# Four small edits in a four-layer image kernel: mask building, first row norm, scaling, and joint-stage statistics

## The chip, the cores and the metric

The kernel runs on one core of a Trainium2 chip, as one program. The metric is device time in microseconds (us) of that core. Engines are named as in the profile: PE (TensorE matmul), PEld (weight loads), DVE (VectorE), ACT (ScalarE), POOL (GpSimd), SP (SyncE, which here only issues DMAs).

## What is computed

Eight images of 56×56 pixels and 192 channels, f32, go through four residual layers, x = x + layer(gn(x)), where gn is a group norm over 32 groups of 6 channels of a whole image:

```python
x = x + L0(gn(x))   # silu(q)*silu(v), Toeplitz mix along rows and columns, gate, output projection
x = x + L1(gn(x))   # LN; shifted-window attention, 7x7 windows, 6 heads, bias + mask; projection
x = x + L2(gn(x))   # W_in (192->384); 3x3 depthwise conv; four EMA scans; LN over 384; W_out
x = x + L3(gn(x))   # 7x7 depthwise conv; LN; 192->768, gelu, 768->192; scaled

# L1, the mask: 64 windows, 49x49 each
attn = einsum(q * scale, k) + bias[None] + mask[None, :, None];  softmax
# L2
proj = x @ W_in + b_in;   local = conv3x3(proj)
mixed = 0.25 * (lr + rl + tb + bt) + local          # scans of local, decay 0.6
out = layernorm_over_channels(mixed) @ W_out + b_out
```

The group norm of a layer needs statistics of the whole image, so every layer's statistics are gathered while the residual of the layer before is added.

## The kernel before

A framework allocates tiles from pools with a number of buffers each, sets the waits from tile to tile, and orders the instructions of each engine, except where the kernel fixes an order itself. Each engine runs its own queue strictly in order. A tile with `bufs=1` can be rewritten only when everything that reads it is done, a DMA out of it included; pools with `bufs=2` and no own number in the call give two buffers. In the profile the stages lie one after another: 0 to 870 q/v projection, 876 to about 2097 the Toeplitz mix, to 3441 attention, 3470 to 3757 layer 2's input projection, to 4385 the depthwise mix, to 4905 the joint stage (layer 2's end with layer 3's beginning), to 5228 the 7×7 convolution, and to 6118 the MLP. The change touches four of them.

**Masks (`build_bias_mask`, L301 to L336).** During the q/v projection (`layer0_qv`: matmuls L371, evacuation with the bias L377 on DVE, silu L378 on ACT, product L379 on DVE), the sums of bias and mask that the attention will add are built in eight chunks and kept in DRAM (`bmask`). Chunk g: POOL clears a tile `mk` (L326) and issues two loads of the mask into it (L328); DVE adds the bias of each of six heads, six instructions (L331), into `bmt`; POOL issues the store to `bmask` (L334). Both `mk` and `bmt` have one buffer. The driver takes chunks from a list (`masks`) between row steps of the projection; in the order that the framework makes of it, all eight stand close together, from 234 to 302 us.

**First norm of the attention (`layer1_norm`, L622 to L662).** A generator for one image, in four row groups g of 392 columns: it scales x (ACT L636), subtracts a mean found by matmul (L644, DVE L646), squares it (ACT L648), sums the squares by matmul (L652) and copies 32 partitions of sums into `rs` (L653). After all four rows comes one square root (ACT L654, with a table load), one reciprocal (DVE L655), then per row a matmul that spreads the factors (`rstd`, L660) and the multiplication (DVE L662). For image 0 the whole generator runs ahead of the first attention block (L1266 to L1269). For the others it is advanced by the letter N of a hand-written plan (L1278), a list of parts whose order PE follows: Q projects queries and keys (L679), V values (L698), E makes weights (scores, max, exp, sum, normalise; L719 to L734; the POOL multiplications L729 and L734 are in it), T transposes them (L754), P multiplies with v, R projects. The parts of image 0's first block run ahead of the plan (L1272 to L1274).

**Input projection (`layer2_in`, L811 to L843; called at L1323 to L1328).** For image b: POOL clears the padding of `xn` (L815), DVE scales the image in three instructions (L818), POOL clears two edge rows (L821, L822), then 15 groups of matmuls (L830) write PSUM tiles `pin` (four buffers), each evacuated with the bias by DVE (L838) into `pt`; at the end SP stores `pt` to `pd` (L843). The next image's load (`layer2_image`, SP, L807 and L808) is issued ahead of it. `x`, `xn` and `pt` have two buffers. After image 5 the last image's group norm is finished (`gn_finish`, L168 to L182), as its sums come last from the attention.

**Joint stage (`layer2_out`, `layer3_in`, loop in the driver).** DVE's order is written out by hand there: the order of the code. An image has 12 places i = 3k + j (four column groups k, three channel groups j). At each: normalised rows `yt` for the next group (DVE L951, ACT L953), the output projection (PE L975), the residual on DVE (L980, into x2o), and pieces of two other chains. One is the layer norm statistics of the next image (`ln_pieces`, DVE L190 on `ml`, 28 pieces of 0.87 us), at i = 3 to 8, and its variance at i = 8. The other is the generator `layer3_in` of the image before: group norm statistics (L144, 12 instructions of 0.55 us), group norm finish (L168 and after), scaling (POOL L1000), transposes (PE L1015) and copies (ACT L1023 to L1027), and the store `zd` (L1028). It is advanced by one step at places i < 5, two from i = 5 on. The transposed normalised rows are copied by ACT into `y` (L963). The load of `ml` for image b+2 is issued on SP at k = 3.

The functions that the diff touches, and what calls them:

Of the kernel before, what the change touches and what calls it, by code (L numbers as in the profile page):

```python
# [10 lines left out]
F32 = mybir.dt.float32  # L11
# [9 lines left out]
TT = 392  # L21
# [56 lines left out]
def kernel(ctx: ExitStack, tc: tile.TileContext, a: dict, out: bass.AP):  # L78
# [222 lines left out]
    def build_bias_mask(psum, pool, masks):  # L301


        rev = pool.tile([WN, WN], F32, name="rev", bufs=1)
        nc.gpsimd.dma_start(rev, a["rev49"])

        raw = pool.tile([WN, HEADS, WN], F32, name="raw", bufs=1)
        tab = a["rel"]
        for i in range(7):
            for h in range(HEADS):  # L310
                nc.gpsimd.dma_start(
                    raw[7 * i:7 * i + 7, h].rearrange("p (i j) -> p i j", i=7),
                    bass.AP(tab.tensor, tab.offset + 13 * i + 169 * h, [[1, 7], [13, 7], [1, 7]]),
                )
        yield
        bt = pool.tile([128, HEADS, WN], F32, name="bt", bufs=1)
        nc.vector.memset(bt, 0.0)
        bp = psum.tile([128, 2, 512], F32, name="bp", tag="qv")[0:WN, 0, 0:HEADS * WN]
        nc.tensor.matmul(bp, rev, raw.rearrange("p h m -> p (h m)"), start=True, stop=True)
        for r in range(2):  # L320
            nc.vector.tensor_copy(bt[64 * r:64 * r + WN].rearrange("p h m -> p (h m)"), bp)
        mask = a["mask"].rearrange("(g q r) n m -> g r n q m", q=4, r=2)

        def eighth(g):
            mk = pool.tile([128, 4, WN], F32, name="mk", bufs=1)
            nc.gpsimd.memset(mk, 0.0)  # L326
            for r in range(2):
                nc.gpsimd.dma_start(mk[64 * r:64 * r + WN], mask[g, r])  # L328
            bm = pool.tile([128, 3, 4, 2, WN], F32, name="bmt", bufs=1)
            for h in range(HEADS):  # L330
                nc.vector.tensor_tensor(  # L331
                    bm[:, h % 3, :, h // 3, :], mk, bt[:, h:h + 1, :].to_broadcast([128, 4, WN]), ALU.add
                )
            nc.gpsimd.dma_start(bmask[g], bm.rearrange("p a b c d -> p (a b c d)"))  # L334

        masks += [lambda g=g: eighth(g) for g in range(8)]  # L336


    def layer0_load(b, pool):
# [279 lines left out]
        rolled(x1[b], x, False, queues)  # L619
        return x  # L620

    def layer1_norm(b, x, pool, psum, consts):  # L622


        ones2, ones32, sel = consts[4:]

        xr = pool.tile([128, 3 * NH + 16], F32, name="xr")
        nc.gpsimd.memset(xr[:, 3 * NH:], 0.0)
        xw = xr[:, 0:3 * NH].rearrange("p (j n) -> p j n", j=3)
        rs = pool.tile([128, TT], F32, name="rs1")  # L630
        yield xr
        sc, sh = scsh1[:, b, 0], scsh1[:, b, 1]
        for g in range(4):
            gs = bass.ts(g, TT)
            for j in range(3):
                nc.scalar.activation(  # L636
                    xw[:, j, gs].rearrange("p (w i j) -> p w i j", i=7, j=7),
                    x[:, j, 7 * g:7 * g + 7].rearrange("p i (w j) -> p w i j", j=7), AF.Identity,
                    bias=sh[:, j:j + 1], scale=sc[:, j:j + 1],
                )  # L640
# [12 lines left out]
            nc.vector.tensor_copy(rs[32 * g:32 * g + 32], vp)  # L653
        nc.scalar.activation(rs, rs, AF.Sqrt, bias=eps5)  # L654
        nc.vector.reciprocal(rs, rs)  # L655
        for g in range(4):
            yield
            gs = bass.ts(g, TT)
            bp = psum.tile([128, 512], F32, name="rstd", tag="mm", bufs=3)[:, 0:TT]
            nc.tensor.matmul(bp, sel[32 * g:32 * g + 32], rs[32 * g:32 * g + 32], start=True, stop=True)  # L660
            xs = xw[:, :, gs]
            nc.vector.tensor_tensor(xs, xs, bp.unsqueeze(1).to_broadcast([128, 3, TT]), ALU.mult)  # L662

    def layer1_scores(g, xr, pool, psum, S, es, consts):

# [142 lines left out]
        queue.dma_start(x[64:128, :, 0:R2 - 3], src[:, :, R2 - 1:H])  # L808
        return x

    def layer2_in(b, x, pool, psum, w_in, b_in):  # L811

        sc, sh = scsh2[:, b, 0], scsh2[:, b, 1]
        xn = pool.tile([128, 3, R2, 64], F32, name="xn2")
# [5 lines left out]
            ))  # L820
        nc.gpsimd.memset(xn[0:64, :, 0, 0:W], 0.0)  # L821
        nc.gpsimd.memset(xn[64:128, :, R2 - 3:R2, 0:W], 0.0)  # L822
        pt = pool.tile([128, C2, P2], F32, name="pt")
        nh = R2 // 2
        for i in range(nh):
            ns = 2 if i + nh < P2 else 1
            ps = psum.tile([128, 2, 512], F32, name="pin")
            for j in range(3):
                for s in range(ns):
                    nc.tensor.matmul(  # L830
                        ps[:, s, 0:C2], xn[64 * s:64 * s + 64, j, 2 * i:2 * i + 2].rearrange("p h w -> p (h w)"),
                        w_in[64 * s:64 * s + 64, j], start=(j == 0), stop=(j == 2),
                    )
# [4 lines left out]
            nc.vector.tensor_tensor(dst, ps[:, 0:ns, 0:C2], b_in[:, v, 0:ns], ALU.add)  # L838

        n = CG2 if b + 1 == nimg else 0  # L840
        if n:
# [123 lines left out]
                bias=vec("be2", m), scale=vec("g2", m),  # L965
            )

    def layer2_out(k, j, y, x, psum, w_out):
# [12 lines left out]


    def layer3_in(b, x, zp, pool, psum):
# [260 lines left out]
    with ExitStack() as st:  # L1244
# [30 lines left out]

# [6 lines left out]
        for b in range(nimg):  # L1282
# [5 lines left out]
            for g in range(4):  # L1288
# [27 lines left out]
    with ExitStack() as st:  # L1316
# [3 lines left out]
        x = [layer2_image(0, xpool, nc.scalar)]  # L1320
        w_in = resident("w_in", nc.scalar, pool)
        b_in = resident("b_in", nc.scalar, pool)
        for b in range(nimg):  # L1323
            if b + 1 < nimg:
                x.append(layer2_image(b + 1, xpool, nc.sync))
            layer2_in(b, x[b], pool, psum, w_in, b_in)
            if b == nimg - 3:
                run(gn_finish(mv2[:, last], scsh2[:, last, 0], scsh2[:, last, 1], pool, psum, "pin"))  # L1328
    with ExitStack() as st:
# [29 lines left out]
        for n in range(-1, len(groups)):  # L1359
# [9 lines left out]
            for j in range(3):  # L1369
# [2 lines left out]
                        rows[0] = ln_rows(*var_next, eps5, pool)  # L1372
                    following = scaled(*after, j)
                if n >= 0:
                    layer2_out(k, j, y, x[b], psum, w_out)
# [10 lines left out]
            if k == 3:  # L1386
                run(steps)
                nc.sync.dma_start(xd[b], x[b])
                steps = layer3_in(b, x[b], zp, pool, psum)
        run(steps)  # L1390


# [133 lines left out]
```

## Time and profile before

| | |
|---|---|
| three runs | 6127.48, 6127.55, 6136.09 us; median 6127.55 |
| the profiled execution | 6119.55 us |
| its span | 6117.8 us, mean granted PE clock 0.943 |
| POOL busy | 1330.2 us (22%) |
| DMA moved | 1013 MB, mean 166 GB/s |
| input projection, 8 blocks | 3469.8 to 3756.7 |
| joint stage, period of an image | 58.4 us (4658.4 to 4716.8 to 4775.2) |

How to read it: the page gives busy times over the whole span; of an edit to one stage they tell little, because the stages have different limits. The groups of instructions ("line engine operation, out<-in, shapes, count | busy, mean ns | idle before <-releaser") tell how long an instruction takes and what it waited for. The windows give the busy times of a stretch with the granted PE clock. The waits give "engine tile line <- releaser: total us, times, longest".

### The profile page before, as it was taken

What the parts mean: (1) busy time and instruction counts of PE and PEld (TensorE: products, weight loads), DVE (VectorE), ACT (ScalarE), POOL (GpSimd) and SP (SyncE); (2) the same over time, 40 slices, a digit from 0 to 9 for tenths busy, and PEclk for the clock granted to TensorE, in tenths of its full rate; (3) what the DMA queues carried; (4) which work ended last, traced back from release to release, by engine and by line L of the source; (5) the groups of instructions that cost most, each with busy time, mean ns of one, the idle gap of its engine ahead of it and who ended that gap; (6) DMA issues with size and microseconds to landing.
All of it is one profiled execution on the core that took longest, in us unless ns stands there. A gap on an engine that the chain in (4) does not pass through costs nothing. (4 is left out here: it accounts for less than half of the span.)

```text
span 6117.8 us, 126576 instructions
## 1 busy us (share of the span) xinstructions
PE 5451.9 (89%) x55636; PEld 3509.4 (57%) x55636; DVE 3401.5 (56%) x4760; ACT 2216.8 (36%) x2938; POOL 1330.2 (22%) x867
## 2 busy tenths in 40 slices
PE   6799989999999888888888687999889889799999
PEld 5576766666666545555555455677544489444444
DVE  5677765565555445455454475888787601433331
ACT  2344444444444333333332101555466610333333
POOL 2100015444445212222222101433201100110100
PEclk8899999999999888999998898999989999899999
DMA  6799986666666614544533475667667588321210
GB/s 163 185 214 215 194 224 260 251 258 257 253 255 259 124 33 65 66 61 65 61 50 53 119 227 192 228 231 236 196 166 223 171 319 326 118 88 58 84 48 24
DMA packets 1034540, 1013.11 MB, mean 166 GB/s; under 512 B 826136, under 2 KB 958196, under 8 KB 1007220
## 3 DMA queue, kind: packets, MB, share of 16 engines
q1 hardware_dynamic: 1019424, 940.93, 54.5%
q0 software_dynamic: 8416, 39.40, 2.0%
q10 hardware_dynamic: 6148, 24.68, 1.3%
q8 instruction: 437, 7.16, 0.5%
q14 instruction: 115, 0.94, 0.0%
HBM read 676.28 MB, written 345.08 MB: 167 GB/s over the span
## 5 line engine op out<-in xcount | busy, mean ns | idle before, releaser
L371 PE MATMUL qv<-w_qv_sb,xn 64*112 64x288 f32 x5376 | 724.6, 426 | 51.1 <-DVE act L377 47.8
L409 POOL COPY lc<-lt 128x896 f32<-128x896 f32 (+1 forms) x320 | 572.7, 1806 | 620.4 <-PE op L417 602.6
L371 PEld LDWEIGHTS qv<-w_qv_sb,xn 64*112 64x112 f32 x5376 | 532.7, 184 | 238.1 <-DVE act L377 64.4
L378 ACT ACTIVATE act<-act 112x576 f32<-112x576 f32 x448 | 300.3, 682 | 462.1 <-DVE act L377 424.4
L1154 PE MATMUL ph<-y,w_sb 64*128 64x392 f32 x2304 | 398.4, 498 | 6.4 <-ACT hid L1158 6.4
L1165 PE MATMUL po<-hid,w_sb 128*64 128x392 f32 x2304 | 386.3, 494 | 0.0
L429 PE MATMUL pj<-xn,w_p_sb 64*128 64x392 f32 (+1 forms) x1920 | 373.4, 515 | 13.8 <-issue 10.5
L417 PEld LDWEIGHTS op<-rc,lc 128*56 128x56 f32 x9216 | 308.1, 136 | 127.1 <-issue 66.1
L417 PE MATMUL op<-rc,lc 128*56 128x56 f32 x9216 | 339.4, 221 | 43.9 <-POOL lc L409 25.7
L450 PE MATMUL y<-pp,w_o_sb 128*64 128x392 f32 (+1 forms) x1920 | 356.2, 504 | 21.9 <-DVE x L458 12.7
L377 DVE TENSOR_TENSOR act<-qv,b_qv 112x576 f32<-112x576 f32 x448 | 320.8, 751 | 90.8 <-PE qv L371 90.4
L1172 DVE TENSOR_TENSOR x<-x,z 128x392 f32<-128x392 f32 x96 | 71.0, 740 | 522.1 <-ACT z L1170 522.1
L409 ACT COPY rc<-rt 128x896 f32<-128x896 f32 (+1 forms) x160 | 256.8, 1605 | 238.7 <-PE op L417 219.8
L881 PE MATMUL cv<-zc,wt 128*128 128x224 f32 x1536 | 312.8, 355 | 24.2 <-DMA zc<-pd 24.2
L881 PEld LDWEIGHTS cv<-zc,wt 128*128 128x128 f32 x1536 | 290.2, 189 | 67.8 <-issue 51.9
L443 DVE TENSOR_TENSOR pp<-pp,ot 128x784 f32<-128x784 f32 (+1 forms) x160 | 154.6, 966 | 313.2 <-ACT pp L434 293.7
L1154 PEld LDWEIGHTS ph<-y,w_sb 64*128 64x128 f32 x2304 | 220.3, 188 | 176.3 <-issue 26.2
L729 POOL TENSOR_TENSOR e<-e,mx 128x1176 f32<-128x1176 f32 x64 | 139.8, 2184 | 812.5 <-DVE mx L728 629.6
L1055 PE MATMUL cps<-zc,wt 128*128 128x224 f32 x1536 | 299.1, 355 | 16.7 <-DMA zc<-zd 15.6
L830 PE MATMUL pin<-w_in_sb,xn 64*128 64x384 f32 x1392 | 251.5, 511 | 60.4 <-POOL xn L821 60.4
L1055 PEld LDWEIGHTS cps<-zc,wt 128*128 128x128 f32 x1536 | 289.0, 189 | 26.9 <-issue 19.4
L679 PE MATMUL qk_ps<-xr,wg 64*96 64x392 f32 x1536 | 299.5, 511 | 0.3 <-ACT oa L780 0.3
(211 smaller groups left out, 9113.6 us busy)
## 6 DMA issues: line engine op xcount, KB each, us to landing
lt<-left SPq DMA_DIRECT2D x72, 1792.0 KB
rt<-right SPq DMA_DIRECT2D x72, 1792.0 KB
left<-qv SPq DMA_DIRECT2D x224, 252.0 KB
right<-qv SPq DMA_DIRECT2D x448, 126.0 KB
wt<-in_band_dram SPq DMA_DIRECT2D x23, 2048.0 KB
wt<-in_band_dram SPq DMA_DIRECT2D x11, 4096.0 KB
zc<-pd SPq DMA_DIRECT2D x187, 232.0 KB
pd<-pt SPq DMA_DIRECT2D x7, 5568.0 KB
```

The lines of the kernel that those rows point to most:

```text
L371: nc.tensor.matmul(ps[s][:, which, 0:D1 // 2], xn[64 * s:64 * s + 64, j, bass.ts(i, 2 * W)], w_qv[64 * s:64 * s + 64, j, which, ns], start ...
L377: nc.vector.tensor_tensor(act, ps[s][:, :, 0:D1 // 2], b_qv[:, :, ns], ALU.add)
L378: nc.scalar.activation(act, act, AF.Silu)
L409: copy(c[:, 0:nu], raw.rearrange("p (w u d) -> p u d w", u=nu, d=64 // nu)[:, :, d0:d0 + 8])
L417: nc.tensor.matmul(op[64 * u:64 * u + W, i, :], lc[:, u, i], rc[:, u, i], start=True, stop=True)
L429: nc.tensor.matmul(ps[0:M, s, 0:TT], w_p[64 * s:64 * s + 64, j, d0:d0 + M], xn[64 * s:64 * s + 64, j, ts], start=(j == 0), stop=(j == 2),)
L450: nc.tensor.matmul(y[64 * s:64 * s + 64], w_o[0:M, c, 64 * j:64 * j + 64], pp[0:M, s], start=(c == gated[0][0]), stop=(c == gated[-1][0]),)
L679: nc.tensor.matmul(ps[s], wg[64 * s:64 * s + 64, j, c0:c0 + HC], xw[64 * s:64 * s + 64, j, gs], start=(j == 0), stop=(j == 2),)
L881: nc.tensor.matmul(dst, wt[:, c4 + i, 128 * q:128 * q + 128], zc[:, :, c4 + i, q:q + NPAIR], start=(q == 0), stop=(q == 1),)
L1055: nc.tensor.matmul(dst.rearrange("p (b n) -> p b n", n=NPAIR), wt[:, c4 + i, q * OP:(q + 1) * OP], zc[:, :, c4 + i, q:q + NPAIR], start=(q ...
L1154: nc.tensor.matmul(ps[:, s, 0:TT], w0[64 * s:64 * s + 64, j, m * 128:(m + 1) * 128], y[64 * s:64 * s + 64, j, ts], start=(j == 0), stop=(j ...
L1165: nc.tensor.matmul(ps[64 * s:64 * s + 64], w1[:, m, 64 * j:64 * j + 64], hid[:, m, s], start=(m == 0), stop=(m == 5),)
```

## The change

It makes four edits.

1. The mask tile gets two buffers; the load of chunk g + 1 is issued ahead of chunk g's additions, and that of chunk 0 when the list is made. `bmt` stays at one buffer.
2. For image 0, each row of `layer1_norm` takes its own square root (straight from PSUM) and reciprocal over 32 partitions, and is scaled at once. The first block's Q parts begin after row 0, and the other rows are advanced between parts and by N.
3. The scaling of layer 2's input (with its three memsets) is a function of its own, run for image b + 1 after the evacuation i = 7 of image b.
4. In the joint stage the group norm's statistics are taken from each residual tile right behind it (nine instructions of 448 columns and three of 224, in place of twelve of 392), so that `layer3_in` loses them and two of its steps. The next image's layer norm pieces lie over places i = 1 to 8, three or four at each; two generator steps are taken from i = 6 on, not 5.

```diff
-        def eighth(g):
-            mk = pool.tile([128, 4, WN], F32, name="mk", bufs=1)
+        def load(g):
+            mk = pool.tile([128, 4, WN], F32, name="mk")
             nc.gpsimd.memset(mk, 0.0)
             for r in range(2):
                 nc.gpsimd.dma_start(mk[64 * r:64 * r + WN], mask[g, r])
+            mks.append(mk)
+
+        def add(g):
             bm = pool.tile([128, 3, 4, 2, WN], F32, name="bmt", bufs=1)
...
-        masks += [lambda g=g: eighth(g) for g in range(8)]
+        load(0)
+        masks += [lambda g=g: (load(g + 1) if g < 7 else None, add(g)) for g in range(8)]
```

```diff
@@ layer1_norm(b, x, pool, psum, consts, first=False)
+        def scaled(g):
+            gs = bass.ts(g, TT)
+            bp = psum.tile([128, 512], F32, name="rstd", tag="mm", bufs=3)[:, 0:TT]
+            nc.tensor.matmul(bp, sel[32 * g:32 * g + 32], rs[32 * g:32 * g + 32], start=True, stop=True)
+            xs = xw[:, :, gs]
+            nc.vector.tensor_tensor(xs, xs, bp.unsqueeze(1).to_broadcast([128, 3, TT]), ALU.mult)
...
-            nc.vector.tensor_copy(rs[32 * g:32 * g + 32], vp)
+            if not first:
+                nc.vector.tensor_copy(rs[32 * g:32 * g + 32], vp)
+                continue
+            rg = rs[32 * g:32 * g + 32]
+            nc.scalar.activation(rg, vp, AF.Sqrt, bias=eps5[32 * g:32 * g + 32])
+            nc.vector.reciprocal(rg, rg)
+            yield
+            scaled(g)
+            yield
+        if first:
+            return
@@ driver
-        steps = layer1_norm(0, x[0], pool, psum, consts)
-        xr = [next(steps)]
-        for _ in steps:
-            pass
+        own = layer1_norm(0, x[0], pool, psum, consts, True)
+        xr = [next(own)]
+        for _ in range(4):
+            next(own)
...
         for part in Q + [E[0], V[0], E[1], V[1]]:
             part()
+            next(own)
...
                     if kind == "N":
+                        next(own, None)
                         next(steps, None)
```

```diff
-    def layer2_in(b, x, pool, psum, w_in, b_in):
+    def layer2_scale(b, x, pool):
...
+        return xn
+
+    def layer2_in(b, xn, pool, psum, w_in, b_in, halfway):
...
             nc.vector.tensor_tensor(dst, ps[:, 0:ns, 0:C2], b_in[:, v, 0:ns], ALU.add)
+            if i == nh // 2:
+                halfway()
@@ driver
+        xn = [layer2_scale(0, x[0], pool)]
         for b in range(nimg):
             if b + 1 < nimg:
                 x.append(layer2_image(b + 1, xpool, nc.sync))
-            layer2_in(b, x[b], pool, psum, w_in, b_in)
+
+            def halfway():
+                if b + 1 < nimg:
+                    xn.append(layer2_scale(b + 1, x[b + 1], pool))
+
+            layer2_in(b, xn[b], pool, psum, w_in, b_in, halfway)
```

```diff
         nc.vector.scalar_tensor_tensor(xs, ps[:, 0:nt], vec("b_out", j), xs, ALU.add, ALU.add)
+        nc.vector.bn_stats(st[:, j, k], xs)
@@ layer3_in(b, x, st, zp, pool, psum)
-        st = pool.tile([128, 3, NTH, 6], F32, name="gh_st")
         mv = pool.tile([128, 1, 3, 2], F32, name="gh_mv")
-        for t in range(NTH):
-            gn_piece(st, x, t)
-            if t % 2:
-                yield
@@ driver
-                    if b + 1 < nimg and 3 <= i < 9:
-                        ln_pieces(st_next, ml[b + 1], range(NPAIR * (i - 3) // 6, NPAIR * (i - 2) // 6))
+                    if b + 1 < nimg and 1 <= i < 9:
+                        ln_pieces(st_next, ml[b + 1], range(NPAIR * (i - 1) // 8, NPAIR * i // 8))
...
-                    for _ in range(1 if i < 5 else 2):
+                    for _ in range(1 if i < 6 else 2):
                         next(steps, None)
```

More of the change, by code (lines that the diff above doesn't have):

```diff
@@ L322, in build_bias_mask @@
         mask = a["mask"].rearrange("(g q r) n m -> g r n q m", q=4, r=2)
-        def eighth(g):
-            mk = pool.tile([128, 4, WN], F32, name="mk", bufs=1)
+        mks = []
+        def load(g):
+            mk = pool.tile([128, 4, WN], F32, name="mk")
             nc.gpsimd.memset(mk, 0.0)
@@ L331, in eighth @@
                 nc.vector.tensor_tensor(
-                    bm[:, h % 3, :, h // 3, :], mk, bt[:, h:h + 1, :].to_broadcast([128, 4, WN]), ALU.add
+                    bm[:, h % 3, :, h // 3, :], mks[g], bt[:, h:h + 1, :].to_broadcast([128, 4, WN]), ALU.add
                 )
             nc.gpsimd.dma_start(bmask[g], bm.rearrange("p a b c d -> p (a b c d)"))
-        masks += [lambda g=g: eighth(g) for g in range(8)]
+        load(0)
+        masks += [lambda g=g: (load(g + 1) if g < 7 else None, add(g)) for g in range(8)]
     def layer0_load(b, pool):
@@ L620, in layer1_load, with layer1_norm @@
         return x
-    def layer1_norm(b, x, pool, psum, consts):
+    def layer1_norm(b, x, pool, psum, consts, first=False):
         ones2, ones32, sel = consts[4:]
@@ L657, in layer1_norm @@
             yield
[L658 to L662, printed above, removed]
+            scaled(g)
     def layer1_scores(g, xr, pool, psum, S, es, consts):
@@ L966, in layer2_turned, with layer2_out @@
             )
-    def layer2_out(k, j, y, x, psum, w_out):
+    def layer2_out(k, j, y, x, st, psum, w_out):
         n0 = 4 * k
@@ L980, in layer2_out, with layer3_in @@
         nc.vector.scalar_tensor_tensor(xs, ps[:, 0:nt], vec("b_out", j), xs, ALU.add, ALU.add)
[L983 removed]
+        nc.vector.bn_stats(st[:, j, k], xs)
+    def layer3_in(b, x, st, zp, pool, psum):
         sc = pool.tile([128, 1, 3], F32, name="sc3")
         sh = pool.tile([128, 1, 3], F32, name="sh3")
[L987 removed]
         mv = pool.tile([128, 1, 3, 2], F32, name="gh_mv")
[L989 to L992 removed]
         gn_aggregate(st, mv[:, 0])
@@ L1374 @@
                 if n >= 0:
-                    layer2_out(k, j, y, x[b], psum, w_out)
+                    if k == j == 0:
+                        gst = pool.tile([128, 3, 4, 6], F32, name="gh_st")
+                    layer2_out(k, j, y, x[b], gst, psum, w_out)
                     i = 3 * k + j
-                    if b + 1 < nimg and 3 <= i < 9:
-                        ln_pieces(st_next, ml[b + 1], range(NPAIR * (i - 3) // 6, NPAIR * (i - 2) // 6))
+                    if b + 1 < nimg and 1 <= i < 9:
+                        ln_pieces(st_next, ml[b + 1], range(NPAIR * (i - 1) // 8, NPAIR * i // 8))
                     if b + 1 < nimg and i == 8:
                         var_next = ln_var(in_halves(st_next), C2, pool)
-                    for _ in range(1 if i < 5 else 2):
+                    for _ in range(1 if i < 6 else 2):
                         next(steps, None)
@@ L1388 @@
                 nc.sync.dma_start(xd[b], x[b])
-                steps = layer3_in(b, x[b], zp, pool, psum)
+                steps = layer3_in(b, x[b], gst, zp, pool, psum)
         run(steps)
```

## Prediction

> **What bounds the kernel now.** I read the page first, then the groups by line, then the waits and windows of the four places that the change touches.
>
> ```profile
> PE 5451.9 (89%) x55636; PEld 3509.4 (57%) x55636; DVE 3401.5 (56%) x4760; ACT 2216.8 (36%) x2938; POOL 1330.2 (22%) x867
> L830 PE MATMUL pin<-w_in_sb,xn 64*128 64x384 f32 x1392 | 251.5, 511 | 60.4 <-POOL xn L821 60.4
> ```
>
> TensorE is busy 89% of the span, so a gain can only come from the 666 us in which it isn't, or from matmuls that run at the half clock after an idle stretch. No edit removes a matmul. The question for each edit is how much PE idleness lies at its place. The largest is at L830, layer 2's input projection: 60.4 us, put down to the last memset of xn, which follows the scaling. The stretch around one such gap:
>
> ```profile
> 3501.42 0.84 DVE L838 TENSOR_TENSOR pt<-pin,b_in_sb 128x384 f32<-128x384 f32 x1 [0.39 <-PE pin L830]
> 3501.51 0.70 POOL L815 MEMSET xn<- 128x720 f32 x1 [30.33 <-PE pin L830]
> 3502.11 3.26 DVE L818 TENSOR_SCALAR xn<-x,scsh 128x1680 f32<-128x1680 f32 x3
> ...
> 3505.42 0.23 POOL L821 MEMSET xn<- 64x168 f32 x1 [3.21 <-DVE xn L818]
> ...
> 3505.71 6.50 PE L830 MATMUL pin<-w_in_sb,xn 64*128 64x384 f32 x30 [4.33 <-POOL xn L821]
> ```
>
> The chain is last evacuation, three scales, memset, first matmul of the next image. The windows (columns: stretch, length, busy of PE, PEld, DVE, ACT, POOL, granted clock, DMA share, GB/s) show what follows the gap, then the rest of the block, then a whole block:
>
> ```profile
> 3505.70:3509.10 3.40, 3.39 (x12) 1.96 (x14) 0.00 (x0) 0.00 (x0) 1.26 (x3) 0.58 0.99 419
> 3509.10:3533.80 24.70, 24.70 (x156) 14.62 (x154) 19.68 (x13) 0.00 (x0) 0.00 (x0) 1.00 0.76 214
> 3505.00:3540.00 35.00, 30.68 (x174) 17.75 (x174) 25.46 (x19) 0.00 (x0) 2.19 (x5) 0.94 0.73 233
> ```
>
> So each gap also costs 3.4 us at a clock of 0.58. The other places, in order: the mask building (waits, 225 to 305), the first layer-1 norm, the joint stage (one steady image), and the end of the joint stage on the chain.
>
> ```profile
> DVE bmt L331 <- DMA mk<-in_mask_dram: 34.6, 7, 7.3
> PEld qv L371 <- DVE act L377: 34.2, 16, 6.4
> ACT xr L636 <- DMA x<-x: 11.5, 1, 11.5
> 4658.40:4716.80 58.40, 51.97 (x305) 26.83 (x302) 45.17 (x84) 39.93 (x59) 6.54 (x9) 0.97 0.72 207
> 4879.32 5.62 DVE gh_st L144 x12
> ```
>
> **Part 1: scaling halfway (the largest).** Block starts in the trace are 3469.83, 3505.71, 3540.72, 3576.98, 3612.19, 3648.56, 3688.98 and 3724.51; the last ends at 3756.7, so eight blocks take 286.9 us. A block at full clock is 87 matmul pairs of 0.3225 us = 28.06. Now image b+1 is scaled after the eighth of 15 evacuations of image b. Its order on DVE is 8 evacuations, 3 scales (3.4 us), 7 evacuations. DVE's work per block is 14 × 1.54 + 0.84 + 3.4 = 25.8 us, under 28.06. The scales queue evacuations behind them: a group needs 1.935 us of PE and 1.54 of DVE; with four PSUM buffers PE has two spare groups (some 4 us) when the scales begin, and DVE is late by 2.9 us at most, recovering 0.4 per group. PE should not stop. POOL's three memsets (1.4 us) move along with it, and POOL does nothing else here. On SP the loads of images 1 to 3 go ahead of the first pd store. A store of 5.57 MB takes about 14.5 us and a load of 2.35 MB about 12: 26.5 of 28.06, so DMA is nearly the next limit. A load has about a block of slack, a store some 30 us (pt has two buffers).
> After: first block 31.55 with its ramp (nothing precedes it), seven of 28.06, and about 7.5 at block 5 to 6, where the group norm of the last image (gh_m, gh_v, sc: 3679.4 to 3685.4) still stands ahead of the scaling: 235.5. Gain **51.4**.
> The Trainium skill ("TensorE: Matmul & The Clock Gate", What's actually happening) says that the clock falls to half after an idle window of about 3.4 us and rises after one busy window of as much: 1.7 us lost per ramp. By it the gain is 7 gaps × (4.8 + 1.7) = 45.5, less what the group norm leaves (5) = 40. The row says more: blocks after a gap take 30.2 to 31.7 from first matmul to last, not 28.06, because the half-clock stretch is 3.4 or 6.8 us long. I take the row, 51, with 40 to 59 as ends.
>
> **Part 2: masks ahead.** Eight chunks start at 234.06 to 299.50, 9.35 us apart: six adds (starts 0.275 apart, 1.65), the bmask store's issue (0.57), a memset (0.28), two mask loads (1.50 to issue, 5 us median to land), then the next adds. Two evacuations follow each chunk on the in-order DVE, and PE stands behind those. In 234.06 to 301.86, 67.8 us, 18 L377 evacuations run; in an equal stretch from 305 it is 36. Lost: 33.9. After, the load lies a chunk ahead, but bmt has one buffer, so adds wait until the bmask store (588 KB) lands, median 4.2 us. A chunk becomes 1.65 + 0.3 + 4.2 + 0.1 = 6.25, and 7 × 6.25 + 1.65 = 45.4 us holds 14 evacuations, worth 26.4: lost 19.0. Gain 14.9. The skill ("DMA: Bandwidth & Descriptors", Anatomy of one DMA) gives 2.0 us + bytes/436e3 for a store from GpSimd's queue: 3.4 us, a chunk of 5.45, gain 19. The row has the transfer beside the stage's own stores, so it decides; at its longest landing (5.4) the gain is 8, with the moved loads sharing the queue 5. Taken: **13** (5 to 20).
>
> **Part 3: first norm row by row.** x arrives at 2125.3; four rows take 7.1 us each, then one square root with its table load (1.28 + 0.62), one reciprocal (2.60), and multiplies; the first L679 matmul is at 2162.45. After, row 0 alone precedes it: the sum of squares is out at 2131.94, sqrt 0.62, reciprocal 2.6 (32 rows cost as much as 128: the L653 copy over 32 partitions takes 0.562 us, L689's over 96 takes 0.562), rstd 0.9, multiply 1.38: 2137.7, 25 us earlier. Added: three reciprocals (7.8 us DVE), three square roots (1.9), four table loads (5.1 ACT). The other rows' 15 us of PE are not saved, only put between the parts. Walking the in-order queues to the second L734 I get 2181 instead of 2194.9, then row 3 inside block 0 gives back 5 (5.0 PE, 5.4 DVE, 6.5 ACT with two reloads). Net **9** (4 to 13).
>
> **Part 4: joint stage.** The period is 58.4 us an image: PE 51.97, DVE 45.17, ACT 39.93, so none is full over the whole, but DVE is from 4672.5 to 4702.4 (the layer norm pieces: 28 × 0.868), and ACT from 4703.6 to 4715. Twelve statistics of 0.553 (6.6 us per image) become twelve of 9 × 0.61 + 3 × 0.36 = 6.6: the same work. Spreading the 28 pieces over eight places relieves the middle (from the second place to the variance 40.1 us, then about 38.5), but the group norm's steps come out a place later, so the zt copies of the last third (3.8 us of ACT) fall ahead of the y copies where ACT is full: the stretch from the variance to the image's end, 12.65, becomes about 14.5. Without a row for that overlap I bound it at ±1.2 us per image over seven images and take 0, its middle. At the very end the 5.62 us burst leaves the chain except its last 0.36: −5.3; and image 0 has early DVE idleness to use (0 to 5, taken 2). Together **7** (25 faster to 8 slower).
>
> **Sum.** 51 + 13 + 9 + 7 = 80. The profiled execution took 6119.55 (span 6117.8 and 1.75 around it) and should take 6039.5; it is 8 us under the median of the runs, 6127.55, so the median should be **6047**.
>
> **Rivals.** (1) The joint stage is really smoothed: DVE's 5.4 us idle at 4710.8 to 4716.2 and its early idleness take the pieces, 2.5 us per image, −18 more: 6029. For it: a full DVE for half the period. Against: ACT's full stretch is untouched. (2) The gains meet their next limits: DMA at 26.5 of 28.06 makes PE wait for xn or pt in some blocks (part 1 gives 42), mask chunks wait 5.4 for the store (part 2: 6), layer 1's start loses its lead to table loads (part 3: 4), the joint stage gives 0: 52, 6076. (3) Slower: the pieces now start at i=1, some 10 us earlier, and stand in DVE's queue ahead of L980. The ml load (issued 4700.71, landing about 4722, first needed 4730.9) must be in by then. If not, each late microsecond holds L980, its two PSUM buffers, and so PE, in seven images. It outweighs the 80 only above (80 + 12)/7 = 13 us per image; at 14 us, 6145. Against: about 5 us of slack remain, the load being issued earlier too. That an edit does nothing is excluded for the scaling: the instruction order has it halfway.
>
> **Numbers.** Forecast 0.58, rival 1 0.17, rival 2 0.22, rival 3 0.03. The range, 6015 to 6080, reaches from all upper bounds of 1 to 3 with rival 1 to the lower bounds of rival 2. A measurement tells 0.2%, 12 us, from no change. Faster 0.95, same 0.03, slower 0.02.
>
> **What would show it.** L830's idle falls from 60 to about 10 and its blocks stand 28.1 apart; DVE's bmt waits for the bmask store, not the mask; the first L679 follows x by 12.5 us, not 37; no burst of twelve L144 before the end; the joint period stays 57 to 60. Wrong if L830 still waits each block, or the period leaves those bounds.

## The result, and the profile after

Median 6096.4 us (6080.9 to 6105.5, 12 runs) against 6128.8 (6110.5 to 6143.5, 12 runs): ratio 0.9943, interval 0.9932 to 0.9953. The forecast was 6047, in a range of 6015 to 6080. The direction was right, the gain less than half of the forecast.

The profiled execution after took 6080.9 us (span 6079.1), 38.7 less in the span than before. Cut at the first or last record of a matmul line, the two traces give:

| stretch | before | after | change | forecast |
|---|---|---|---|---|
| start to the last q/v matmul | 869.4 | 854.7 | −14.7 | −13 |
| Toeplitz mix (untouched) | 1228.0 | 1221.0 | −7.0 | 0 |
| attention, to its last projection | 1342.3 | 1337.4 | −4.9 | −9 |
| wait ahead of the input projection | 30.2 | 29.4 | −0.8 | 0 |
| input projection, eight blocks | 286.9 | 243.1 | −43.7 | −51 |
| to the last conv matmul of layer 2 | 613.3 | 614.4 | +1.1 | 0 |
| to the last output matmul of the joint stage | 508.8 | 546.6 | **+37.8** | −2 |
| from there to the 7×7 convolution | 43.2 | 36.9 | −6.3 | −5 |
| the rest | 1195.7 | 1195.6 | −0.1 | 0 |

Three edits did about what was said; the joint stage took most of it back. (The untouched mix took 1218 to 1238 in the profiles of the experiments, so its −7.0 is a difference between executions, not part of the change.)

The page and the groups of the changed kernel, whose L856 was L830:

```profile
PE 5467.6 (90%) x55636; PEld 3528.8 (58%) x55636; DVE 3412.2 (56%) x4759; ACT 2223.2 (37%) x2945; POOL 1321.6 (22%) x867
L856 PE MATMUL pin<-w_in_sb,xn 64*128 64x384 f32 x1392 | 237.5, 491 | 29.4 <-POOL xn L843 29.4
```

L856's idle time is down from 60.4 to 29.4, which is the single wait for the first image (30.2 of the 60.4 before). And PE was busy 15.7 us *longer* in all, with as many matmuls and L856 itself 14.0 shorter: elsewhere some 30 us of matmul time was added, and more matmul time without more matmuls points to a lower clock. The timeline of a block and the windows of two:

```profile
3459.96 1.53 DVE L864 TENSOR_TENSOR pt<-pin,b_in_sb 128x768 f32<-128x768 f32 x1 [0.39 <-PE pin L856]
3461.34 3.25 DVE L840 TENSOR_SCALAR xn<-x,scsh 128x1680 f32<-128x1680 f32 x3
3464.50 8.60 DVE L864 TENSOR_TENSOR pt<-pin,b_in_sb 128x768 f32<-128x768 f32 x6
```

```profile
3471.00:3500.03 29.03, 29.03 (x177) 21.45 (x174) 24.75 (x19) 0.00 (x0) 2.19 (x5) 1.00 0.87 281
3500.03:3529.06 29.03, 29.03 (x175) 21.45 (x174) 24.78 (x19) 0.00 (x0) 2.19 (x5) 1.00 0.86 279
```

The three scales stand in the middle of the evacuations, and PE runs through two blocks without a stop at a clock of 1.00. The waits in the mask stage (225 to 305), those at the attention's start (2075 to 2180), and the chain at the end of the joint stage:

```profile
DVE bmt L336 <- DMA bmask<-bmt: 16.3, 6, 4.8
PEld qv L378 <- DVE act L384: 25.6, 16, 5.2
```

```profile
ACT xr L652 <- DMA x<-x: 21.2, 2, 11.0
```

```profile
4846.63 0.46 DVE x2o L1009
4847.11 0.39 DVE gh_st L1010
4847.51 0.17 DVE gh_mv L148
```

DVE now waits for the bmask store, 16.3 us, where it waited 34.6 for the mask, and PE's weight loads wait 25.6 for DVE, not 34.2. The attention still begins with a wait for x in two parts, of 11.0 and 10.2 us; before, over the same stretch, they were 10.9 and 11.5. At the end one statistic of 0.39 us stands where the burst of 5.62 stood. Last, a steady image of the joint stage, and four neighbouring stretches of 3.41 us out of it:

```profile
4668.06:4732.88 64.82, 58.67 (x302) 29.37 (x302) 45.72 (x83) 40.01 (x59) 5.85 (x9) 0.89 0.69 197
```

```profile
4671.37:4674.78 3.41, 3.41 (x28) 2.56 (x27) 2.13 (x7) 0.72 (x1) 0.00 (x0) 1.00 0.79 313
4674.78:4678.20 3.42, 3.42 (x12) 2.01 (x12) 3.34 (x7) 2.23 (x3) 0.00 (x0) 0.50 1.04 441
4678.20:4681.61 3.41, 3.41 (x12) 1.44 (x10) 0.00 (x0) 1.45 (x2) 3.25 (x2) 0.50 0.59 254
4681.61:4685.02 3.41, 3.41 (x20) 1.45 (x20) 1.43 (x3) 2.37 (x3) 1.93 (x4) 1.00 0.17 20
```

The image takes 64.8 us, not 58.4, and its clock is 0.89, not 0.97. PE has 6.1 us without work, as before (6.4); its busy time is what grew, 51.97 to 58.67. In the first of the four stretches PE is busy throughout and at full clock, and yet the clock is halved for the next two. What it did there is mostly matmuls of one column: some 20 of the 28 of the group norm's finish (L168), which now fall at places 0 and 1, where they fell at 2 and 3. The periods, from image to image at the first residual, and the half-clock time in each:

| us | image 0 | 1 | 2 | 3 | 4 | 5 | 6 | 7 (to last residual) | sum |
|---|---|---|---|---|---|---|---|---|---|
| before | 65.7 | 61.0 | 54.0 | 59.6 | 58.4 | 58.4 | 58.3 | 45.9 | 461.3 |
| of it at half clock | 23.9 | 10.2 | 0 | 10.2 | 3.4 | 3.4 | 3.4 | 0 | 54.6 |
| after | 74.8 | 58.2 | 62.4 | 61.6 | 60.6 | 64.8 | 64.8 | 48.9 | 496.2 |
| of it at half clock | 30.7 | 3.4 | 6.8 | 6.8 | 3.4 | 13.7 | 13.7 | 6.8 | 85.3 |

If PE is what limits these stretches, half of the added 30.7 us at half clock, 15, is lost time (an estimate). Image 0, 9.1 us longer, is in part a second term.

### The profile page after: what moved, and what is told of

Read it like the earlier page. It is cut to its first block, busy times and chain, and to the rows that moved or that the text cites. A ratio compares the mean times of both kernels' runs of the same rounds, so it can differ in the third digit from the quotient of the medians.

```text
span 6079.1 us, 126571 instructions
## 1 busy us (share of the span) xinstructions
PE 5467.6 (90%) x55636; PEld 3528.8 (58%) x55636; DVE 3412.2 (56%) x4759; ACT 2223.2 (37%) x2945; POOL 1321.6 (22%) x867
## 5 line engine op out<-in xcount | busy, mean ns | idle before, releaser
L378 PEld LDWEIGHTS qv<-w_qv_sb,xn 64*112 64x112 f32 x5376 | 515.7, 182 | 236.9 <-DVE act L384 54.6
L457 PE MATMUL y<-pp,w_o_sb 128*64 128x392 f32 (+1 forms) x1920 | 355.1, 503 | 20.7 <-DVE x L465 12.5
L1197 DVE TENSOR_TENSOR x<-x,z 128x392 f32<-128x392 f32 x96 | 67.4, 702 | 525.6 <-ACT z L1195 525.6
L1080 PE MATMUL cps<-zc,wt 128*128 128x224 f32 x1536 | 299.1, 355 | 16.4 <-DMA zc<-zd 15.3
L701 PE MATMUL qk_ps<-xr,wg 64*96 64x392 f32 x1536 | 299.1, 511 | 1.5 <-DVE xr L645 1.5
L1004 PE MATMUL po<-y,w_out_sb 128*64 128x448 f32 (+1 forms) x1152 | 286.9, 537 | 7.2 <-DVE x2o L1009 7.0
```

Of the source, the lines that this page charges most:

```text
L378: nc.tensor.matmul(ps[s][:, which, 0:D1 // 2], xn[64 * s:64 * s + 64, j, bass.ts(i, 2 * W)], w_qv[64 * s:64 * s + 64, j, which, ns], start ...
L457: nc.tensor.matmul(y[64 * s:64 * s + 64], w_o[0:M, c, 64 * j:64 * j + 64], pp[0:M, s], start=(c == gated[0][0]), stop=(c == gated[-1][0]),)
L1004: nc.tensor.matmul(ps[64 * s:64 * s + 64, 0:nt], w_out[:, m, 64 * j:64 * j + 64], y[:, m, s, 0:nt], start=(m == 0), stop=(m == 2),)
L1080: nc.tensor.matmul(dst.rearrange("p (b n) -> p b n", n=NPAIR), wt[:, c4 + i, q * OP:(q + 1) * OP], zc[:, :, c4 + i, q:q + NPAIR], start=(q ...
```

## The experiments

Times are ratios to the kernel before, measured on the same chip; "stage" is the joint stage, first to last residual (461.3 before, 496.2 after).

| kernel | ratio | interval | stage | period of image 5 |
|---|---|---|---|---|
| parts 1 to 3, old joint stage | 0.9901 | 0.9885 to 0.9917 | 460.8 | 58.3 |
| + pieces over eight places | 0.9970 | 0.9961 to 0.9980 | 508.0 | 67.4 |
| + statistics with each residual | 0.9920 | 0.9906 to 0.9933 | 480.1 | 59.2 |
| changed kernel (both) | 0.9943 | 0.9932 to 0.9953 | 496.2 | 64.8 |
| both, finish two steps later | 0.9967 | 0.9955 to 0.9980 | 510.0 | 64.9 |
| the same, finish's matmuls widened | 0.9939 | 0.9924 to 0.9953 | 486.3 | 61.3 |
| the same (not widened), step ahead of pieces | 0.9918 | 0.9905 to 0.9932 | 482.4 | 59.9 |
| changed, widened, image 0 as before | 0.9921 | 0.9908 to 0.9934 | 480.2 | 62.7 |
| pieces over eight, zd from ACT's queue | 1.0005 | 0.9997 to 1.0014 | 519.9 | 72.8 |

**1. The old joint stage.** The residual's statistics, `layer3_in`, the places and the step rule as before; parts 1 to 3 stay.

```diff
-        nc.vector.bn_stats(st[:, j, k], xs)
...
-                    if b + 1 < nimg and 1 <= i < 9:
+                    if b + 1 < nimg and 3 <= i < 9:
```

> The changed kernel with the joint stage of before (parts 1 to 3 alone). In the changed kernel's trace the joint stage, first to last residual, is 496.2 us against 461.3 before. Theory J (the joint-stage edit costs about what the other three gain): the stage returns to 461 +- 3, the span to about 6047, and the median to about 6063 (ratio 0.989). Rival N (the joint stage is long in that trace by chance of the run): the stage lies anywhere from 455 to 495 and the median stays near 6096 (ratio 0.995).

The stage took 460.8, the span was 6037.5 (10 below the 6047 expected), the ratio 0.9901. The joint-stage edit costs some 0.4%, and parts 1 to 3 alone are worth 1.0%. Rival N falls.

**2 and 3. Each half of part 4 alone.** First, on the kernel of 1, the pieces over eight places with the old burst; then, on the changed kernel, the pieces back at six places with the statistics at each residual.

```diff
-                    if b + 1 < nimg and 3 <= i < 9:
-                        ln_pieces(st_next, ml[b + 1], range(NPAIR * (i - 3) // 6, NPAIR * (i - 2) // 6))
+                    if b + 1 < nimg and 1 <= i < 9:
+                        ln_pieces(st_next, ml[b + 1], range(NPAIR * (i - 1) // 8, NPAIR * i // 8))
```

> Parts 1 to 3, and of part 4 only the layer norm pieces over eight places; group norm statistics in the old burst and generator steps. Theory G (the loss comes from the group norm's finish, now at places 0 and 1, which strings out its one-column matmuls and drops the clock): images 1 to 6 stay at 58.4 +- 1.5 each, image 0 pays for the early need of ml (about +9), the stage is about 470. Rival L (the early layer norm pieces hold the residuals): images 1 to 6 are at 61 to 65, the stage at 485 to 500.

```diff
-                        ln_pieces(st_next, ml[b + 1], range(NPAIR * (i - 1) // 8, NPAIR * i // 8))
+                        ln_pieces(st_next, ml[b + 1], range(NPAIR * (i - 3) // 6, NPAIR * (i - 2) // 6))
```

> The changed kernel with the layer norm pieces back at places 3 to 8; the statistics stay with each residual, so the group norm's finish stays at places 0 and 1. Theory G: images 1 to 6 stay at 61 to 65 with a half-clock stretch around places 1 to 2, image 0 returns to about 66; stage 480 to 490. Rival L: images return to 58.4, the stage to 458 to 463.

508.0 and 480.1. The pieces alone cost 47 us and the statistics alone 19; together it is 35. My theory that only the finish's place was guilty fell with the first: there the finish is where it always was, and images 2 to 6 take 66 to 67 us, 17 of them at half clock. The statistics alone came out at the edge of what theory G said (480 to 490) and above what rival L allowed (458 to 463): both halves do harm. PE's wait in the kernel before, the waits in the kernel with the pieces alone, and DVE's timeline at the place there say how the pieces do it:

```profile
PE gh_m L168 <- DVE gh_mv L148: 0.8, 4, 0.2
```

```profile
PE gh_m L168 <- DVE gh_mv L148: 17.4, 7, 6.3
DVE ln_st L190 <- DMA ml<-md: 7.0, 5, 2.0
```

```profile
4605.29 2.42 DVE L190 BATCH_NORM_STATS2 ln_st<-ml 112x6 f32<-112x384 f32 x3 [0.98 <-DMA ml<-md]
4607.63 2.89 DVE L144 BATCH_NORM_STATS2 gh_st<-x2o 128x6 f32<-128x392 f32 x6
4610.44 0.66 DVE L1008 SCALAR_TENSOR_TENSOR x2o<-po,vecs_sb,x2o 128x448 f32<-128x448 f32 x1
4611.02 3.10 DVE L190 BATCH_NORM_STATS2 ln_st<-ml 112x6 f32<-112x384 f32 x4
4614.05 0.48 DVE L148 BATCH_NORM_AGGREGATE gh_mv<-gh_st 128x2 f32<-128x24 f32 x3
```

The group norm's aggregate (L148) now has seven layer norm pieces ahead of it in DVE's written order, 5.5 us, and PE, in its own order, already stands at gh_m, which waits for it: 11 us in six waits, where it was 0.8 before. (The longest of the seven, 6.3, is the last image's, behind the end of the stage.)

**4. The finish back at its old places.** Two empty steps ahead of the finish, so that it falls at places 2 and 3 again.

```diff
     def layer3_in(b, x, st, zp, pool, psum):
+        yield
+        yield
         gn_aggregate(st, mv[:, 0])
...
-                    for _ in range(1 if i < 6 else 2):
+                    for _ in range(1 if i < 5 else 2):
```

> The changed kernel with two empty steps ahead of the group norm's finish (and two steps per place from place 5 on again), so that the finish falls at places 2 and 3 as before, with statistics at each residual and layer norm pieces over eight places. Theory G: no half-clock stretch at places 1 to 2, images 1 to 6 at 57 to 60, only image 0 long (about 75): stage 468 to 475. Rival L: 61 to 65 as in the changed kernel, stage 490 or more.

Stage 510.0: worse, not better, and very regular (64.9 per image, 17.1 at half clock). So theory G, as put there, is false: it isn't that the finish is early. The windows around the finish in this kernel, each one period of the clock's decision:

```profile
4628.56:4631.97 3.41, 2.46 (x14) 0.72 (x10) 3.38 (x6) 0.19 (x1) 0.00 (x0) 1.00 0.60 253
4631.97:4635.38 3.41, 2.72 (x19) 2.11 (x20) 1.74 (x9) 0.00 (x0) 0.00 (x0) 1.00 0.00 0
4635.38:4638.80 3.42, 3.42 (x13) 2.34 (x12) 3.39 (x6) 0.00 (x0) 0.00 (x0) 0.50 0.00 0
...
4642.21:4645.62 3.41, 3.41 (x11) 1.44 (x12) 3.41 (x5) 1.72 (x3) 3.41 (x3) 0.50 0.00 0
4645.62:4649.04 3.42, 3.42 (x23) 1.88 (x20) 0.92 (x3) 1.51 (x3) 0.42 (x1) 1.00 0.48 116
```

PE's busy share is 80% in the second, and three windows at half follow. In it 0.32 of the time is matmuls of many columns; the rest of "busy" is one-column gh_m and gh_v. This gave theory K: the clock of a window follows from how much PE streamed in the one before, and one-column matmuls don't count. (A period of 64.9 us is 19.0 such windows, so all these images meet the grid at the same phase: the 17.1 of each is one case repeated.)

**5. Widening the one-column matmuls**, in the kernel of 4: the moving operand is repeated to 64 columns, column 0 is used.

```diff
-                        ps[:, :, j], gmath[:, 2 * k + j, :], v[:, :, k], start=(k == ks[0]), stop=(k == ks[-1])
+                        ps[:, j], gmath[:, 2 * k + j, :], v[:, 0, k:k + 1].to_broadcast([128, 64]),
+                        start=(k == ks[0]), stop=(k == ks[-1])
```

> The kernel with two empty steps ahead of the group norm's finish, and its 28 one-column matmuls per image widened to 64 columns (column 0 is used; the others are copies). Theory K (the clock of a 3.41 us window is halved when PE streamed less than about half of the window before, and one-column matmuls count for nothing): the half-clock stretch that follows the group norm matmuls (onsets after windows in which they fill half of the time) is gone in images 1 to 6, a period falls from 64.9 to 58 to 61, the stage from 510 to 475 to 485; the stretch after the variance stays. Rival W (it is the waiting of PE for gh_mv and ml itself, not which matmuls run): onsets stay, the period stays at 64 to 66, the stage at 505 to 515.

Stage 486.3, period 61.3, half clock 6.8 us per image for 17.1. That is just above K's ranges and far from W's. More arithmetic made the kernel faster by 0.3%. I had expected the onset (the full-clock window that a half-clock one follows) to vanish, and it did not: with PE's wait of 1.64 us for gh_mv in it, that window is filled to 0.52 even with the widened matmuls counted, and the clock still falls. The stretch shrank from 10.2 to 3.4 us: the window behind the onset, full only if the widened matmuls are counted (0.59 to 0.95 without them), restores the clock in five images. K holds for what counts, not for the onset.

**6. The changed kernel, widened, with image 0's pieces at places 3 to 8.**

```diff
+                    if b + 1 < nimg and (1 if b else 3) <= i < 9:
+                        p0, np_ = (1, 8) if b else (3, 6)
```

> The changed kernel with the group norm matmuls widened in the same way, and with image 0's layer norm pieces (on image 1's ml) back at places 3 to 8, all others at 1 to 8. Theory K with the late ml of image 0 as its second term: no half-clock stretch at places 1 to 2 in images 5 to 7 (64.8 becomes 59 to 62), image 0 falls from 74.8 to 65 to 70, the stage from 496 to 474 to 484. Rival W: images 5 and 6 stay at 64 to 65; if only image 0 changes the stage is 486 to 491.

480.2: image 0 67.1 (from 74.8), images 5 and 6 62.7 and 61.2 (from 64.8), with no half clock at place 1 in any of them (images 4 and 5 still drop at place 3). Both terms are borne out, in one profile; image 5 lies just above the range. But the stage stays 19 us above the old one, as with the statistics alone (480.1). Image 0's term is seen on the chain of the changed kernel:

```profile
4328.86 35.73 DMA ml<-md
4364.60 0.02 issue
4364.62 2.36 DVE ln_st L190 x3
```

**7. Rival 3 of the prediction, more directly.** In the kernel of 2 the ml load is issued at +49 to +50 us of an image, behind the second of three zd stores in SP's queue (the expectation below says the third). The zd stores are moved to ACT's queue.

```diff
-            nc.sync.dma_start(zd[b][:, 64 * j:64 * j + 64], zt)
+            nc.scalar.dma_start(zd[b][:, 64 * j:64 * j + 64], zt)
```

> The kernel with layer norm pieces over eight places and the old burst of statistics, whose joint stage took 508.0 us, with the zd stores issued from ACT's queue in place of SP's, so that the ml load is not queued behind them. Theory M (the early pieces wait for ml, whose load is issued on SP behind the third zd store at +50 us of an image and lands some 23 us later): the ml load goes out at about +40, no piece waits for it after image 0, the half-clock stretch at places 2 to 4 shrinks, and the period falls from 67 to 59 to 62, the stage to 470 to 485. Rival D (burst and pieces together hold DVE at places 1 to 3 whenever ml comes): the period stays at 64 to 67, the stage above 495.

A miss, and half inconclusive; the stage is where rival D had it. The ml load went out at +36 to +38, no piece waited for it after image 0, and places 1 to 3 fell from 16.2 us to 13.2 in image 5; but zt's buffers then waited for the zd stores (ACT zt <- DMA zd: 31.9 us in four waits), at places 10 to 11, and the stage was 519.9. Images 4 and 6, which escape that wait, take 63.1. The late ml explains some 3 us per image of 9; the rest was not taken apart in this kernel.

**8. The order.** In the kernel of 4, DVE takes the generator's step before the pieces of the place, not after.

```diff
+                    for _ in range(1 if i < 5 else 2):
+                        next(steps, None)
                     if b + 1 < nimg and 1 <= i < 9:
...
-                    for _ in range(1 if i < 5 else 2):
-                        next(steps, None)
```

> The kernel with two empty steps ahead of the group norm's finish (stage 510.0, period 64.9, gh_mv at place 2 behind four layer norm pieces, PE without work for 4.6 us there), with one change: at each place DVE takes the generator's step before the layer norm pieces, not after them. Theory O (the loss is the order: PE's group norm matmuls wait for DVE's pieces, the window falls under half and the clock drops): gh_mv comes 3 us earlier, the half-clock time per image falls from 17 to 7 to 10 us, the period to 59 to 62, the stage to 475 to 490. Rival D (pieces at early places cost this wherever they stand): the period stays at 64 to 66.

482.4, and in images 1 to 6 half clock 0 to 10 us, period 59.7 to 60.5. Two lines in another order gain 28 us of the stage. gh_mv comes 10.0 to 10.6 us into an image and not 13.0, and PE's wait for it fell from 10.9 us to 1.1. Theory O holds for this kernel; 21 us over the old stage remain.

**9. Part 3 undone**, on the kernel of 1.

```diff
-        own = layer1_norm(0, x[0], pool, psum, consts, True)
-        xr = [next(own)]
-        for _ in range(4):
-            next(own)
+        steps = layer1_norm(0, x[0], pool, psum, consts)
+        xr = [next(steps)]
+        for _ in steps:
+            pass
```

> Parts 1 and 2 alone: the joint stage of before and the first attention norm as before. Theory: part 3 was worth 5 to 13 us, so from the end of the Toeplitz mix to the attention's last projection it takes 1342 +- 4 as before, against 1328 with part 3 alone of the same joint stage; the median is 5 to 13 us above 6045 when scaled to the same kernel before. Rival: the earlier start of the first block is given back in the block: 1328 +- 4 here too, no difference in time.

The attention took 1339.3 from the end of the mix to its last projection (1342.3 before); the twelve kernels with part 3 took 1321.7 to 1344.0, mean 1332.0. Against the mean of the two without, 1340.8, part 3 is worth 9; single executions scatter by more than that. The ratio, 0.9908, is 13 us above that of the next kernel (0.9886), which has 6.8 us of its own at the end; the 7 that are left agree with it without settling it.

**10. The statistics inline for the last image only**, on the kernel of 1.

```diff
+        if st is not None:
+            nc.vector.bn_stats(st[:, j, k], xs)
...
+                        gst = pool.tile([128, 3, NTH, 6], F32, name="gh_st") if b + 1 == nimg else None
```

> Parts 1 to 3 with the joint stage of before, and the statistics with each residual for the last image only. Theory: the burst of twelve statistics at the end (5.6 us) leaves the chain except its last 0.4, images 0 to 6 stay as before: from the last residual to the first 7x7 convolution matmul 43.4 becomes 38; the median falls by 5 below parts 1 to 3 alone. Rival: the last image loses as much inside (48.9 us there against 45.9 in the changed kernel): no difference.

Ratio 0.9886 (0.9871 to 0.9902), stage 461.0, and from the last output matmul to the first convolution matmul 36.7 for 43.5. The end's gain can be had without the stage's loss.

**11 and 12. The best version, with and without part 4.** To the kernel of 10: two buffers for bmt, and the last image's group norm ahead of the first block. Then the same with all of part 4, amended by 5, 6 and 8.

```diff
-            bm = pool.tile([128, 3, 4, 2, WN], F32, name="bmt", bufs=1)
+            bm = pool.tile([128, 3, 4, 2, WN], F32, name="bmt")
...
+        run(gn_finish(mv2[:, last], scsh2[:, last, 0], scsh2[:, last, 1], pool, psum, "pin"))
         xn = [layer2_scale(0, x[0], pool)]
...
-            if b == nimg - 3:
-                run(gn_finish(mv2[:, last], scsh2[:, last, 0], scsh2[:, last, 1], pool, psum, "pin"))
```

> Parts 1 to 3 and the statistics with each residual for the last image only, and besides: two buffers for bmt, and the last image's group norm finish ahead of the first block of the input projection, in the wait for its image, not between blocks 6 and 7. Theory: all seven later blocks are 29.03 us apart, the projection 242 becomes 236; the additions of the masks no longer wait for the bmask store, so that stage ends 3 to 10 us earlier; the median is 9 to 16 us under that of the same kernel without these two. Rival: the mask chunks then wait for POOL's own queue (store issue, memset, two load issues: 2.6 us a chunk) and the stage gains under 2; the projection as said: 6 to 8 us.

> All that was found, with the whole of part 4 kept: parts 1 to 3, two buffers for bmt, the last image's group norm ahead of the input projection, statistics with each residual, pieces over eight places but six for image 0, two empty steps, the generator's step before the pieces, widened group norm matmuls. Theory O: images 1 to 6 at 57 to 60, image 0 at 65 to 69, the joint stage 455 to 466, the median within 8 of 6024 (the same with the old joint stage). Rival D: the stage 475 or more, the median above 6038.

The first is the fastest of all: 6024.0 us, ratio 0.9852 (0.9838 to 0.9865). All later blocks are 29.03 apart, the projection takes 234.0. The mask stage ended at 849.5 against 848.4 in the kernel of 10, so the second bmt buffer gained nothing that shows, and DVE waits for the mask again (16.4 us): the rival's figure came out there. With part 4 amended: stage 479.4, ratio 0.9892. Forecast 455 to 466; a miss, and the stage lies where rival D had it: early pieces cost something in this order too. With at most 6.8 us at half clock each of images 1 to 6 still takes 59.9 to 61.7. Place 2 to 3 takes 8.8 there against 4.4 before, with DVE waiting 2.2 us per image for gh_m, in order ahead of its pieces. What remains of the difference I did not take apart.

## Why the prediction was wrong

**Failed: part 4, the step "the same work … I bound it at ±1.2 us per image … and take 0".** It measured +35 in the stage. The bound counted DVE and ACT time and left the granted clock at 0.97. The relief that it counted on did not come: the middle of an image, from the second place to the variance, was to fall from 40.1 us to 38.5, and took 40.3 in image 4, where no half clock falls into it, and 43.5 in images 5 and 6, where 6.8 us of it are at half clock. The end, worked as 14.5, took 14.1 to 15.1. And the group norm's steps did not come out "a place later": its aggregate runs 1.3 us into these images, where it ran at 10.8.

What makes up the 35: some 12 us are half clock in images 1 to 7 (half of the added 23.9, an estimate). Image 0, which was to gain 2, lost 9.1, with a wait of 8.8 for ml. The other 14 or so lie mainly at places 0 to 2, where the finish's steps now are: the first two take 6.2 and 6.1 us for 5.6 and 4.65 in image 4 even without half clock. Experiment 1 shows that the edit to the joint stage is the cause, 2 and 3 that neither half is free. In the kernel of 4, 30 us above the statistics alone, widening (5) takes back 24 and the order of two lines on DVE (8) takes back 28, each by itself. In the changed kernel itself widening and image 0 as before (6) take back 16. The other 19 stay open, but for some 7 that half clock would still explain (68.3 us of it, 54.6 before; an estimate). Nothing in part 4 asked what PE streams in 3.41 us when a DVE step that PE stands behind comes later, though part 1 had just priced such a stretch.

**Rival 3** named the ml wait. It came in image 0 (8.8 us), where I had not looked: there the load has no image ahead of it to hide in. In later images of the changed kernel the load is in time. As the whole of a slower case it was the wrong mechanism.

**Part 1: the mechanism right, one term mis-sized.** I took a block as 87 matmul pairs, 28.06. But the six records of its last group (64-row matmuls, like the others) have no partner, and each takes the time of a pair: (84 + 6) × 0.3225 = 29.03, as every undisturbed block shows. That is 6.8 of the 7.7 us missing. The group norm's break after block 6 stayed, 6.2 us over 29.03, and the block behind it, partly at half clock, took 2.8 more; the forecast had 7.5 for both, and experiment 11 removed both. The sign "idle falls from 60 to about 10" came out at 29.4, since I had read all 60.4 as gaps between blocks: seven gaps of 4.3 are 30.2 of it, the first image's wait the rest. Rival 2's 42 is near by luck: in the undisturbed blocks PE did not stop for DMA. The clock gate's rule gave 40 and the row 51, on both sides of 43.7; the rule (the Trainium skill, "TensorE: Matmul & The Clock Gate", What's actually happening) asks for an idle window of 3.4 us, and the measurements below decide against that: less idleness is enough.

**Part 2: right.** 14.7 for a worked 14.9 and a taken 13; the new last wait is the store, and with that removed (11) it is the mask load again. Two figures beside it were mis-summed: by the same sum a chunk of 5.45 gives 20.5, not 19, and a landing of 5.4 gives 6.5, not 8.

**Part 3: right**, as far as the scatter allows: the first L701 came 12.6 us after the last part of x (2102.41 to 2115.03), forecast 12.5; net about 9 between the means of twelve kernels and two, 4.9 in the one trace.

**The end:** −6.3 for −5.3.

Summed: 51 became 43.7, 7 became −31.5 (+37.8 and −6.3), the mix gave 7 by chance.

## What to carry to other kernels

Where an engine's order is written by hand, ask of every step that is moved not only what it costs, but who stands behind it on another engine: in the kernel of 2, seven cheap statistics ahead of one aggregate came with a half-clock stretch of TensorE in five images. Judge a spread of work by the profile's granted clock of the stage and not by busy totals; here PE's busy time grew with the same matmuls, and the clock showed why. And take single parts of a bundle apart: three of the four edits here gained 1.0% and the fourth lost 0.4.

## What the runs showed of the hardware

Every change of the granted clock lies on a fixed grid of 3.413 us, of the same phase through a whole execution and another in each. I counted all grid windows of the joint stage in the profiles of 14 kernels by the share of the window in which matmuls of more than one column ran. Of 1653 windows at full clock, all 123 under 0.40 were followed by a half-clock window, 28 of 54 between 0.40 and 0.50, and 11 of 1476 above, five of these being the onsets at 0.52 of experiment 5. Of 311 at half clock, 133 of 135 under 0.95 were followed by another at half, 16 of 176 above. So it needs no idleness of 3.4 us to lose the clock here: in 104 of the 162 windows that lost it, no gap between matmuls was as long as that. To regain it PE had to stream through nearly a whole one. Twelve windows at full clock were over 70% "busy" by the profile but under 0.40 without one-column matmuls; all twelve lost the clock. Since the grid's phase differs by execution, whether a window falls under half is partly luck: the same code took 0 to 10.2 us at half clock in images 1 to 6 of experiment 8. That may be part of why runs of one kernel spread (6080.9 to 6105.5 us after); no run shows it.
